# Adding the message bias of the first two pairs on GpSimd, and reordering the first loads, in a two-layer graph network kernel

## The chip, the cores and the metric

The kernel runs on one core of a Trainium2 chip, in one launch. A core has TensorE for matrix products (PE in the profile; its weight loads are shown apart as PEld), VectorE (DVE), ScalarE (ACT), GpSimd (POOL) and SyncE (SP, which here only issues DMAs). The metric is the device time of one execution in microseconds (us), as the median over several runs; less is better.

## What is computed

64 graphs of 256 nodes with 256 channels go through two layers. All data is float32. Layer 0 joins a convolution along the nodes, a message passing weighted by distance, and a gated recurrent unit; layer 1 is a graph convolution. Each ends in a residual and a normalisation. Cut to what matters:

```python
# layer 0
xc = jnp.transpose(x, (0, 2, 1))
h = relu(bn1(conv1d(xc, conv1_w, 0)))            # 1 tap
h = bn2(conv1d(h, conv2_w, 8))                   # 17 taps
x_conv = jnp.transpose(relu(h + xc), (0, 2, 1))
s = x @ w_se.T + b_se                            # 3 coordinates a node
dist = sq[:, :, None] + sq[:, None, :] - 2.0 * jnp.einsum('bnd,bmd->bnm', s, s)
A = jnp.exp(-dist) * mask                        # mask is adj
msg = relu(x @ w_msg.T + b_msg)
x_nmp = jnp.einsum('bnm,bmd->bnd', A, msg)
gi = concat([x_conv, x_nmp]) @ w_ih.T + b_ih;  gh = x @ w_hh.T + b_hh
r = sigmoid(gi_r + gh_r);  z = sigmoid(gi_z + gh_z);  nn_ = tanh(gi_n + r * gh_n)
x = _layernorm(x + (1.0 - z) * nn_ + z * x)
# layer 1
h = layer_norm(x, ln_gamma, ln_beta)
agg = jnp.einsum('bij,bjh->bih', adj, h)
x = _layernorm(x + x + relu(agg @ W_rel + b_rel + h @ W_root))
```

`sq` is the sum of the squares of `s`; `bn1` and `bn2` are a scale and a shift for each channel.

## The kernel before

**Staging.** The 64 graphs are worked on in 32 pairs, and the convolution in 8 batches of 4 pairs (`BG = 8` graphs). The 17-tap convolution is done in a transformed domain: a batch's activations (tile `XF`) go through butterflies on DVE (`split`, `merge`, lines 611 to 677), products with transformed filters on PE (`product`, L735), and butterflies back. The filters themselves are transformed at the start of the program (`filters`, lines 529 to 596): pieces of the filter weights are loaded (`wt`, L550), laid out by DVE (`ws`, L560), transposed on PE (L569), copied out by ScalarE (L571), multiplied with a small matrix (`ps_w`, L590) and copied into `w2all` by ScalarE (L596). Batch 0 uses `w2all` directly. It is also stored to DRAM (`w2m`, `store_w2`, L527), and from batch 1 on three filters at a time are loaded back into one of two buffers (`cs`, L728), whenever the products of the set before the last have read theirs.

**The first convolution** (`conv1`, 1 tap). For two graphs at a time `x` is loaded (L827), transposed on PE in two halves of the channels (L845, each half four transposes into one PSUM bank), copied out by ScalarE (L846), multiplied with the weights `w1` (L866), and scaled, shifted and passed through a ReLU by ScalarE (L870). The scale and shift come from the channel table `chan` by a few small instructions on DVE and GpSimd (lines 516 to 520). Batch 0's first convolution is the first work of the program. ScalarE issues the loads of `chan` (L494), `w1` (L495) and the small matrix `taps` (L499) in this order; SP issues those of `x`.

**A pair** (`pair(p)`). The message product has 260 columns for a tile of 128 nodes: 256 message channels, 3 coordinates and one of zeros. `xT` times `wms` takes two products, over the two halves of the channels (L1105), into one PSUM bank. The bias `bms` is a tile with the same 260 columns in every partition. For most pairs DVE adds it on the way out of PSUM (L1112). For pairs 0 and 1 (`idle`) a third product adds it, a row of ones times one row of the bias (L1108), and ScalarE copies the bank out (L1110). Then ScalarE takes the coordinates (L1114) and applies the ReLU (L1116), GpSimd makes the squared norms (lines 1119 to 1123), DVE transposes the coordinates (L1126), two DMA round trips place them (L1130, L1135), and the distance products follow (L1142), the exponential (L1146), the mask (L1149) and the sum over neighbours (L1156). The convolution's result is `xc` (L930, L1162, L1163). The gates (L1194 for pairs 0, 1 and 31; L1208 for the others) multiply `xT`, the neighbour sums and `xc` with blocks `WB`, which for pair 0 are loaded (L1043) into the memory that `w2all` has given up. Layer 1 follows with L1383 and L1397.

**What sets the order.** The program is recorded as a list of operations, each with a key, and a planner (`scheduled`, lines 321 to 416) sorts them: it goes through time with assumed durations, DMA rates and PSUM banks, and gives each engine the ready operation of the smallest key. Keys come from the constants at the top: `FIRST_GATES` is the planned time of pair 0's gates and `PERIOD` that of a pair; the others place the loads, the convolution of the next batch, the coordinates (`COORDS`), layer 1's normalisation and projection (`W_LAG`, `LATE_LAG`), the filter stores (`STORES_AT`), or raise the priority of an operation on DVE (`PAIR_LEAD`, `FILTER_LEAD`). Each engine and each DMA queue then works in that fixed order and waits on semaphores. Any change of a constant or an operation can reorder all queues.

Of the kernel before, what the change touches and what calls it, by code (L numbers as in the profile page):

```python
# [18 lines left out]
P = 128  # L19
B, N, D = 64, 256, 256  # L20
C = D // P
# [10 lines left out]
BG = 8  # L32
# [22 lines left out]
OB, OG = 3, 64  # L55
HQ = 2 * M * C * (M + 1)
XC_SLOTS = BG + 2
FIRST_GATES, PERIOD, GATE_TIME = 115.6, 58.9, 14.5
AHEAD_FROM, AHEAD_TO, W_DEEP = -43.5, -52.5, 2
CONV1_FROM, CONV1_TO, CONV_FROM, CONV_OUT, CONV_TO = -29.4, 98.8, -11.5, -38.6, -37.2  # L60
PAIR_LEAD, FILTER_LEAD, LOAD_AHEAD = 40.6, -2.5, 17.5
SMALL_RUNS, TURN_FROM = 1.3, 2
FILTERS_TO, STORES_AT = 51.5, 52.7
KEEP = 13.3
LATE_LAG = 28.4
W_FROM, W_LAG = 2, 41.9
COORDS = 40.5
PLAIN, SUMS_FROM = (0, 1, B // 2 - 1), 2


# [349 lines left out]
def gnn_two_layers(  # L420
# [18 lines left out]
    prog = Program()  # L439
    PE, V, A, G, SP = prog.tensor, prog.vector, prog.scalar, prog.gpsimd, prog.sync  # L440
# [3 lines left out]
    def sb(name, shape, pool="const"):  # L444
        s = Space(name, shape, pool)
        s.after = opened.get(pool)
        spaces[pool].append(s)
        return s.view
# [4 lines left out]
    def bank(name, share="rest"):  # L453
        return Space(name, [P, 512], "psum", share, share if share in ("conv", "gate") else None).view
# [22 lines left out]
    w1 = sb("w1", [P, C, D])  # L477
    mhalf = sb("mhalf", [P, 8])
    ones = sb("ones", [P, P])
    ident = sb("ident", [P, P])  # L480
# [10 lines left out]
    taps = sb("taps", [P, NM * OB], "filters")  # L491

    prog.at(0.0)
    A.dma_start(out=chan_sb, in_=chan)  # L494
    A.dma_start(out=w1, in_=w1T.rearrange("(c p) n -> p c n", p=P))  # L495
    tb = np.zeros((2, OG, NM * OB), np.float32)
    tb[:, :TAPS * OB] = np.einsum("kf,op->kofp", tap_matrix(), np.eye(OB, dtype=np.float32)).reshape(TAPS * OB, NM * OB)
    tb = tb.reshape(P, NM * OB)
# [294 lines left out]
    def fold(q):  # L793
        g0, g1 = 2 * q, 2 * q + 2
        for j, r in ((0, 8), (8, 0)):
            hv = HP[:, q, j:j + 8].rearrange("p j c g k -> p (j c) g k")
            for first, op in ((V0 + r, ALU.subtract), (U + r, ALU.add)):
                o = sl(first, 8).rearrange("p s (c e) -> p (s c) e", c=C)[:, :, g0 * M:g1 * M]
                V.tensor_tensor(o.rearrange("p s (g t) -> p s g t", t=M), hv[:, :, :, 0:M], hv[:, :, :, 1:M + 1], op)

    def hd(p):
        return h_dram[p].rearrange("f p e -> (f p e)")[:P * HQ].rearrange("(p e) -> p e", p=P)

    def conv1(b):
        def edges(h):
            G.memset(h[:, :8, :, :, M:], 0.0)
            G.memset(h[:, 8:, :, :, :1], 0.0)
        XN = {}

        def fetch(g):  # L810
            if b >= TURN_FROM:
                XN[g] = xn_ahead[:, :4 * D]
                blocks = XN[g].rearrange("p (c k i) -> p c k i", c=C, i=SQ)
                rows_of = x[b * BG + g:b * BG + g + 2].rearrange("g (b j) d -> j (g b) d", j=SQ)
                with prog.group():
                    for a in range(P // SQ):
                        for c in range(C):
                            at = c * P + a * SQ
                            SP.dma_start(out=blocks[a * SQ:(a + 1) * SQ, c], in_=rows_of[:, :, at:at + SQ])
                return  # L820
            if b > 0:
                XN[g] = xn_ahead[:, :4 * D].rearrange("p (j d) -> p j d", d=D)
            elif g >= 4:
                XN[g] = W2[:, 1, 8 + 2 * g:12 + 2 * g]
            else:
                XN[g] = cs[:, g * 512:g * 512 + 1024].rearrange("p (j d) -> p j d", d=D)
            SP.dma_start(out=XN[g], in_=x[b * BG + g:b * BG + g + 2].rearrange("g (c p) d -> p (g c) d", p=P))  # L827

        def turned(g):
            xn = XN[g]  # L830
            if b >= TURN_FROM:
                V.transpose(xTc_ahead.rearrange("p c n -> p (c n)"), xn)
                SP.dma_start(out=xt_dram[(b * BG + g) // 2], in_=xTc_ahead)
                return xTc_ahead
            if b > 0 or g == 4:
                xTc = xTc_ahead
            elif g:
                xTc = W2[:, 1, 6 * g - 12:6 * g - 8].rearrange("p (c f) o -> p c (f o)", c=C)
            else:
                xTc = cs[:, 2048:3072].rearrange("p (c n) -> p c n", c=C)  # L840
            for c in range(C):
                ps = bank("ps_xTc")
                with prog.group():
                    for j in range(4):
                        PE.transpose(ps[:, j * P:(j + 1) * P], xn[:, j, c * P:(c + 1) * P], ident, hold=[xTc[:, c]])  # L845
                A.copy(xTc[:, c, :], ps)  # L846
            SP.dma_start(out=xt_dram[(b * BG + g) // 2], in_=xTc)
            return xTc

        if b == 0:  # L850
            for g in range(0, BG, 2):
                fetch(g)
                edges(HP[:, g // 2])
        for g in range(0, BG, 2):
            h = HP[:, g // 2]
            if b > 0:
                fetch(g)
            xTc = turned(g)
            if b > 0:
                h = xn_ahead.rearrange("p (j c g k) -> p j c g k", j=M, c=C, g=2)  # L860
                edges(h)
            for o in range(C):
                ps = bank("ps_c1")
                with prog.group():
                    for c in range(C):
                        PE.matmul(ps, w1[:, c, o * P:(o + 1) * P], xTc[:, c, :], start=(c == 0), stop=(c == C - 1),  # L866
                                  hold=[h[:, :, o]])
                pv = ps.rearrange("p (g t j) -> p j g t", g=2, j=M)
                for j, at in ((0, 0), (8, 1)):
                    A.activation(h[:, j:j + 8, o, :, at:at + M], pv[:, j:j + 8],  # L870
                                 AF.Relu, bias=bn_shift[0][:, o:o + 1], scale=bn_scale[0][:, o:o + 1])
            if b == 0:
                fold(g // 2)
            else:
                SP.dma_start(out=hd(b * BG // 2 + g // 2), in_=xn_ahead)
# [88 lines left out]
    bms = sb("bms", [P, D + 4])  # L964
# [38 lines left out]
    msg = sb("msg", [P, 2, C, D + 4], "ahead")  # L1003
# [5 lines left out]
    def keep(steps, key):  # L1009
        for q in range(BG // 2):  # L1010
            prog.at(key + KEEP * q)
            next(steps, None)
# [44 lines left out]
    ps = bank("ps_hrow")  # L1057
# [10 lines left out]
    ps = bank("ps_mean")  # L1068
# [17 lines left out]
    def pair(p):  # L1086
# [12 lines left out]
        idle = p < 2  # L1099
        for g in range(2):  # L1100
            for m in range(C):
                ps = bank("ps_msg")
                with prog.group():
                    for c in range(C):
                        PE.matmul(ps[:, :D + 4], xT[:, c, g, m * P:(m + 1) * P], wms[:, c, :], start=(c == 0),  # L1105
                                  stop=(c == C - 1 and not idle), hold=[msg[:, g, m]])
                    if idle:
                        PE.matmul(ps[:, :D + 4], ones[0:1, :], bms[0:1, :], start=False, stop=True)  # L1108
                if idle:
                    A.copy(msg[:, g, m], ps[:, :D + 4])  # L1110
                    continue
                V.tensor_add(msg[:, g, m], ps[:, :D + 4], bms)  # L1112
        for m in range(C):
# [10 lines left out]

        prog.at(due - COORDS, 0.3)
        V.transpose(turned.rearrange("p m e -> p (m e)"), st.rearrange("p m e -> p (m e)"))  # L1126
        placed = s_dram[p % 2].rearrange("q (f n) -> (q f) n", n=N)[:16]
        with prog.group():
            for a in range(P // SQ):
                SP.dma_start(out=placed.rearrange("f (m b i) -> f m b i", m=C, i=SQ)[:, :, a, :],  # L1130
                             in_=turned[a * SQ:a * SQ + 16])
# [5 lines left out]
        pss = [bank("ps_dist") for _ in range(2 * C)]  # L1137
        with prog.group():
            for g in range(2):
                for m in range(C):  # L1140
                    r = slice((2 * g + m) * SR, (2 * g + m) * SR + 4)
                    PE.matmul(pss[2 * g + m][:, :N], lr[r, 0, m * P:(m + 1) * P], lr[r, 1, :], start=True, stop=True,  # L1142
                              hold=[AT[:, g, m]])
# [7 lines left out]
        for g in range(2):  # L1151
            ps = bank("ps_nmp")
            with prog.group():
                for d in range(C):
                    for m in range(C):
                        PE.matmul(ps[:, d * N:(d + 1) * N], msg[:, g, m, d * P:(d + 1) * P], AT[:, g, m, :],  # L1156
                                  start=(m == 0), stop=(m == C - 1), hold=[nmp[:, :, g]])
# [100 lines left out]
        else:  # L1258
            for T in (RG, ZN):
# [10 lines left out]
                d = bank("ps_d", "gate")  # L1270
# [17 lines left out]
        for some in pieces:  # L1288
            r, gh, z, n = (T[:, some, h, :] for T in (RG, ZN) for h in range(2))
# [77 lines left out]
        def project(gs, q):  # L1367
            prog.at(due + 2 * GATE_TIME + (8 if not apart else -6 if gs[0] else 13 - 2 * GATE_TIME) + (0.0 if apart or p < W_FROM else LATE_LAG if late else W_LAG), 0.6)
            if apart:
# [17 lines left out]
        def aggregate(gs):  # L1387
            prog.at(due + 2 * GATE_TIME + (16 if not apart else 14 - 2 * GATE_TIME) + (0.0 if apart or p < W_FROM else LATE_LAG if late else W_LAG), 0.4)
            q, sh = next(q3s), next(shs)
# [71 lines left out]
    for b in range(NB):  # L1461
# [11 lines left out]
        if b + 1 < NB:  # L1473
            start, span = FIRST_GATES + b * BG // 2 * PERIOD, BG // 2 * PERIOD
# [99 lines left out]
```

## Time and profile before

| | us |
|---|---|
| median of 3 runs (1989.74 to 1990.74) | 1990.72 |
| the profiled execution's own time | 1990.39 |
| its span, first to last instruction | 1988.6 |
| PE busy | 1974.2 |
| DVE busy | 1710.0 |
| ScalarE busy | 1006.7 |
| GpSimd busy | 275.3 |
| one-row products (L1108), 16 passes, busy | 5.6 |
| mean granted TensorE clock | 0.999 |

A float32 product appears as two passes, so the 8 one-row products are 16 rows on PE. A timeline line has start, duration, engine, line, operation, output and inputs, shape and count; in brackets stand the idle time before it and what ended that. A line of a stretch has its bounds, its length, and the busy time of PE, PEld, DVE, ACT and POOL with their counts, then the granted clock, the busy share of the DMA engines and GB/s. SPq and ACTq are the times that an engine's queue took to issue a DMA; when a transfer has landed is read from the sixteen semaphore updates that each makes. Busy times overlap, and idle time of an engine that does not set the end costs nothing.

### The profile page before, as it was taken

The numbers are of one execution on the slowest core, as the hardware profiler recorded it, in microseconds if no ns is written. First come the engines' busy times: TensorE is split into PE (matmuls) and PEld (weight loads), VectorE is DVE, ScalarE is ACT, GpSimd is POOL, SyncE is SP. The second block draws the span as 40 slices with busy tenths as digits, with TensorE's granted clock in tenths as the row PEclk, the third lists the DMA queues.
The fourth block names the chain that finished last, engine by engine and source line by source line (L and its number), as shares of the span: only waits on it lengthen the run. The fifth ranks groups of instructions, "written<-read, shape, count | busy, mean of one in ns | idle before, by whom it ended". The sixth has DMA issues, their size and how long they took to land.

```text
span 1988.6 us, 28895 instructions
## 1 busy us (share of the span) xinstructions
PE 1974.2 (99%) x10212; PEld 1604.6 (81%) x10212; DVE 1710.0 (86%) x2674; ACT 1006.7 (51%) x2342; POOL 275.3 (14%) x504
## 2 busy tenths in 40 slices
PE   9999999999999999999999999999999999999998
PEld 6887789777887788878887788877888788887875
DVE  6896998999989999899998999899988999985655
ACT  7545342754456543475345644475444653465432
POOL 1000110210110211111110111111111021111101
PEclk9999999999999999999999999999999999999999
DMA  8954555446545465445553545544554334422221
GB/s 219 309 169 127 139 170 140 126 108 186 136 141 149 110 184 143 130 132 135 184 153 109 142 140 171 146 136 112 156 149 150 99 84 158 126 77 77 76 54 43
DMA packets 461089, 273.14 MB, mean 137 GB/s; under 512 B 258192, under 2 KB 445584, under 8 KB 460944
## 3 DMA queue, kind: packets, MB, share of 16 engines
q1 hardware_dynamic: 460384, 270.94, 47.1%
q8 instruction: 81, 1.33, 0.3%
q14 instruction: 64, 0.52, 0.1%
q10 hardware_dynamic: 560, 0.34, 0.1%
HBM read 194.01 MB, written 77.20 MB: 136 GB/s over the span
## 4 chain that ended last, share of the span: by engine, by line
PE 97%; ACT 1%; DVE 1%; DMA 1%; issue 0%; SPq 0%; POOLq 0%; POOL 0%; ACTq 0%; DVEq 0%
PE ps_a L1208 22%; PE ps_k L735 17%; PE ps_d L1208 11%; PE ps_hy L1383 11%; PE ps_c L866 6%; PE ps_nmp L1156 6%; PE ps_msg L1105 6%; PE ps_b L1208 6%; PE ps_agg L1397 5%; PE ps_g L1194 5%; PE ps_dist L1142 1%; ACT w2all L596 1%; PE ps_w L590 1%; ACT tT L571 0%; DMA w<-in_w1T_dram 0%
## 5 line engine op out<-in xcount | busy, mean ns | idle before, releaser
L735 PEld LDWEIGHTS ps_k<-XF,cs 128*128 128x128 f32 x2632 | 311.8, 192 | 14.7 <-issue 8.7
L735 PE MATMUL ps_k<-XF,cs 128*128 128x128 f32 x2632 | 313.3, 275 | 0.0
L1383 PE MATMUL ps_hy<-wrr,wT 128*128 128x512 f32 x496 | 226.8, 595 | 0.0
L1208 PE MATMUL ps_a<-nmp,WB 128*128 128x256 f32 x696 | 207.0, 379 | 0.0
L1383 PEld LDWEIGHTS ps_hy<-wrr,wT 128*128 128x128 f32 x496 | 91.6, 190 | 89.8 <-issue 83.0
L1208 PE MATMUL ps_a<-tx,WB 128*128 128x256 f32 x522 | 156.0, 381 | 2.0 <-ACT ZN L1220 2.0
L1222 ACT ACTIVATE RG<-ps_a,bhh 128x512 f32<-128x512 f32 x116 | 79.2, 683 | 142.8 <-PE ps_a L1208 140.6
L1208 PEld LDWEIGHTS ps_a<-nmp,WB 128*128 128x128 f32 x696 | 132.2, 190 | 18.0
L1220 ACT COPY ZN<-ps_a 128x512 f32<-128x512 f32 x116 | 67.6, 582 | 149.4 <-PE ps_a L1208 148.8
L707 DVE TENSOR_TENSOR XF<-XF 128x512 f32<-128x512 f32 (+3 forms) x128 | 125.8, 1002 | 10.0 <-ACT XF L788 8.6
L1105 PE MATMUL ps_msg<-wms,xT 128*128 128x260 f32 x512 | 133.2, 383 | 0.0
L1156 PE MATMUL ps_nmp<-AT,msg 128*128 128x256 f32 x512 | 118.8, 379 | 0.0
L1385 DVE SCALAR_TENSOR_TENSOR HY<-ps_hy,q,hrow 128x512 f32<-128x512 f32 x124 | 92.7, 748 | 30.2 <-PE ps_hy L1383 24.9
L1397 PE MATMUL ps_agg<-HY,adja 128*128 128x256 f32 x504 | 117.2, 379 | 0.0
L1208 PEld LDWEIGHTS ps_a<-tx,WB 128*128 128x128 f32 x522 | 96.5, 190 | 24.7 <-issue 9.3
L1397 PEld LDWEIGHTS ps_agg<-HY,adja 128*128 128x128 f32 x504 | 95.1, 190 | 23.6 <-issue 10.9
L1156 PEld LDWEIGHTS ps_nmp<-AT,msg 128*128 128x128 f32 x512 | 96.8, 190 | 15.9 <-issue 2.9
L1105 PEld LDWEIGHTS ps_msg<-wms,xT 128*128 128x128 f32 x512 | 94.7, 190 | 14.9 <-issue 2.6
L866 PE MATMUL ps_c<-xTc,w 128*128 128x512 f32 x232 | 105.9, 594 | 0.0
L1208 PE MATMUL ps_a<-xc,WB 128*128 128x256 f32 x348 | 103.5, 379 | 0.0
L1208 PE MATMUL ps_a<-tc,WB 128*128 128x256 f32 x348 | 103.5, 379 | 0.0
L1208 PE MATMUL ps_d<-nmp,WB 128*128 128x256 f32 x348 | 103.5, 379 | 0.0
(226 smaller groups left out, 4254.7 us busy)
## 6 DMA issues: line engine op xcount, KB each, us to landing
cs<-w2m SPq DMA_DIRECT2D x105, 768.0 KB
adjm<-in_adjT_dram SPq DMA_DIRECT2D x64, 256.0 KB
xT<-xt SPq DMA_DIRECT2D x32, 512.0 KB
adja<-in_adjT_dram SPq DMA_DIRECT2D x64, 256.0 KB
out_dram<-HY SPq DMA_DIRECT2D x63, 256.0 KB
hd<-xn SPq DMA_DIRECT2D x28, 544.0 KB
XF<-hd SPq DMA_DIRECT2D x28, 544.0 KB
xt<-xTc SPq DMA_DIRECT2D x29, 512.0 KB
```

What stands on the lines that cost most here:

```text
L707: (V.tensor_add if add else V.tensor_sub)(sl(o, n), sl(a, n), sl(b, n))
L735: PE.matmul(ps[:, o * P:(o + 1) * P], w(m, c)[:, o * P:(o + 1) * P], X[:, slot, c * P:(c + 1) * P], start=first and o == 0 and c == 0, sto ...
L866: PE.matmul(ps, w1[:, c, o * P:(o + 1) * P], xTc[:, c, :], start=(c == 0), stop=(c == C - 1), hold=[h[:, :, o]])
L1105: PE.matmul(ps[:, :D + 4], xT[:, c, g, m * P:(m + 1) * P], wms[:, c, :], start=(c == 0), stop=(c == C - 1 and not idle), hold=[msg[:, g, m]])
L1156: PE.matmul(ps[:, d * N:(d + 1) * N], msg[:, g, m, d * P:(d + 1) * P], AT[:, g, m, :], start=(m == 0), stop=(m == C - 1), hold=[nmp[:, :, g]])
L1194: PE.matmul(ps[:, h * N:(h + 1) * N], block[:, s, gate, :], right[s][2 * k + g], start=0 in ks and h == 0 and s == sources[0] and k == 0, ...
L1208: PE.matmul(ps[:, h * N:(h + 1) * N], block[:, s, gate, :], right[s][at], start=start and h == 0 and j == 0, stop=j == len(sources) - 1, s ...
L1220: A.copy(o, ps)
L1222: A.activation(o, ps, AF.Identity, bias=bhh[:, 2, f:f + 1])
L1383: PE.matmul(ps, wT[:, 2 * f + g, m * P:(m + 1) * P], wrr[:, f, :], start=(f == 0), stop=(f == C - 1), hold=[HY[:, g, m]], need=[q[:, 1, j: ...
L1385: stt(HY[:, g, m, :], ps, q[:, 1, j:j + 1], hrow)
L1397: PE.matmul(ps[:, n_ * D:(n_ + 1) * D], adja[:, g, m, n_ * P:(n_ + 1) * P], HY[:, g, m, :D], start=(m == 0), stop=(m == C - 1))
```

## The change

Four things change. For pairs 0 and 1 the one-row product is gone: ScalarE copies the bank out, and GpSimd then adds the bias in SBUF, one instruction of 128x260 for each of the eight tiles. The load of `w1` is issued ahead of that of `chan`. The load of the first two graphs of `x` is split into one for each graph, and their transposes are grouped by graph, so that each of two PSUM banks gets two transposes from the first graph and two from the second; both copies follow. And eleven of the planner's constants have new values, which reorders the queues of all engines through most of the program.

```diff
-FIRST_GATES, PERIOD, GATE_TIME = 115.6, 58.9, 14.5
-AHEAD_FROM, AHEAD_TO, W_DEEP = -43.5, -52.5, 2
+FIRST_GATES, PERIOD, GATE_TIME = 112.8, 58.9, 14.5
+AHEAD_FROM, AHEAD_TO, W_DEEP = -31.4, -60.1, 2
...
-PAIR_LEAD, FILTER_LEAD, LOAD_AHEAD = 40.6, -2.5, 17.5
+PAIR_LEAD, FILTER_LEAD, LOAD_AHEAD = 40.4, 0.1, 17.5
...
-FILTERS_TO, STORES_AT = 51.5, 52.7
-KEEP = 13.3
-LATE_LAG = 28.4
-W_FROM, W_LAG = 2, 41.9
-COORDS = 40.5
+FILTERS_TO, STORES_AT = 51.4, 46.6
+KEEP = 13.0
+LATE_LAG = 28.1
+W_FROM, W_LAG = 2, 43.3
+COORDS = 39.9
...
+    A.dma_start(out=w1, in_=w1T.rearrange("(c p) n -> p c n", p=P))
     A.dma_start(out=chan_sb, in_=chan)
-    A.dma_start(out=w1, in_=w1T.rearrange("(c p) n -> p c n", p=P))
...
-            SP.dma_start(out=XN[g], in_=x[b * BG + g:b * BG + g + 2].rearrange("g (c p) d -> p (g c) d", p=P))
+            for k in range(2) if b == 0 and g == 0 else ():
+                SP.dma_start(out=XN[g][:, 2 * k:2 * k + 2], in_=x[k].rearrange("(c p) d -> p c d", p=P))
+            if b > 0 or g > 0:
+                SP.dma_start(out=XN[g], in_=x[b * BG + g:b * BG + g + 2].rearrange("g (c p) d -> p (g c) d", p=P))
...
-            for c in range(C):
+            if b == 0 and g == 0:
+                pss = [bank("ps_xTc") for _ in range(C)]
+                for k in range(2):
+                    with prog.group():
+                        for c in range(C):
+                            for j in (2 * k, 2 * k + 1):
+                                PE.transpose(pss[c][:, j * P:(j + 1) * P], xn[:, j, c * P:(c + 1) * P], ident,
+                                             hold=[xTc[:, c]])
+                for c in range(C):
+                    A.copy(xTc[:, c, :], pss[c])
+            for c in range(C) if b > 0 or g > 0 else ():
...
-                                  stop=(c == C - 1 and not idle), hold=[msg[:, g, m]])
-                    if idle:
-                        PE.matmul(ps[:, :D + 4], ones[0:1, :], bms[0:1, :], start=False, stop=True)
+                                  stop=(c == C - 1), hold=[msg[:, g, m]])
                 if idle:
                     A.copy(msg[:, g, m], ps[:, :D + 4])
+                    G.tensor_add(msg[:, g, m], msg[:, g, m], bms)
                     continue
```

## The prediction

> **What bounds the kernel now.** I read the page's busy times and chain first, then stretches of the span, the list of who waited for whom, and the timelines of the places that the diff touches.
>
> ```profile
> PE 1974.2 (99%) x10212; PEld 1604.6 (81%) x10212; DVE 1710.0 (86%) x2674; ACT 1006.7 (51%) x2342; POOL 275.3 (14%) x504
> PE 97%; ACT 1%; DVE 1%; DMA 1%; issue 0%; SPq 0%; POOLq 0%; POOL 0%; ACTq 0%; DVEq 0%
> 60.00:90.00 30.00, 29.07 (x208) 22.98 (x206) 28.48 (x46) 12.65 (x31) 0.26 (x2) 1.00 1.06 351
> 90.00:120.00 30.00, 30.00 (x249) 27.64 (x248) 24.64 (x39) 10.54 (x22) 1.73 (x7) 1.00 0.29 101
> 600.00:1500.00 900.00, 900.00 (x4542) 732.45 (x4541) 814.32 (x1234) 466.01 (x1112) 133.75 (x240) 1.00 0.50 142
> ```
>
> The second number of a stretch is its length, the third PE's busy time, the fifth DVE's. PE never rests from 66 us to 1580 us, at a granted clock of 1.00, so an instruction taken off PE there is time taken off the end, as long as what feeds PE can come earlier too. PE's idle time is 14.4 us (1988.6 - 1974.2): some 3 us before 7.1 us, 1.3 us up to 66 us, 2 us between 1580 and 1950 us, the rest at the end. In the instruction order of the two built programs the last 231 merged rows of PE are equal, and 224 of DVE's, so I leave the end as it is.
>
> **The one-row products (L1108) go.** Four groups of two passes for each of pairs 0 and 1:
>
> ```profile
> 80.78 1.04 PE L1105 MATMUL ps_msg<-wms,xT 128*128 128x260 f32 x4
> 81.75 0.70 PE L1108 MATMUL ps_msg<-bms,ones 1*128 1x260 f32 x2
> 82.38 1.98 PE L866 MATMUL ps_c<-xTc,w 128*128 128x512 f32 x4
> ...
> 382.60 1.04 PE L1105 MATMUL ps_msg<-wms,xT 128*128 128x260 f32 x4
> 383.47 0.59 PE L1208 MATMUL ps_a<-xT,WB 128*128 128x256 f32 x2
> ```
>
> From start to start a message tile takes 1.60 us with the one-row product (80.78 to 82.38) and 0.87 us without it, as later pairs do (382.60 to 383.47). The difference, 0.73 us, is more than two more passes of the same width (0.43): PE's weight load also waits 0.34 us at the change of rows. 8 x 0.73 = **5.8 us** off a PE that is full.
>
> In their place come eight GpSimd adds of 128x260 behind ScalarE's copies. No such add is in the trace. Below, the nearest rows are 0.20 us (128x4 add beside an idle DVE), above 1.38 us (the 128x1536 memset, L543) and 1.79 us (the power of 128x8, L1358); I take 1.0 us, between them. They lie off PE: POOL is busy 1.7 us of 90 to 120 us. Behind them wait the coordinates of a pair (L1114 to L1135), then its distance products. Pair 0: last message tile copied at 89.8, distances at 118.0; the built order still leaves 27.5 us of PE work between. Pair 1: 30 us. One add in series is hidden in either, and would have to last over 5 us to show.
>
> **Weights and x at the start.**
>
> ```profile
> 1.18 0.55 ACTq L495 DMA_DIRECT2D w<-in_w1T_dram  x1
> 5.00 1.15 PE L845 MATMUL ps_xTc<-ident,cs 128*128 128x128 f32 x8
> 5.74 1.07 ACT L846 COPY cs<-ps_xTc 128x512 f32<-128x512 f32 x2 [2.10 <-PE ps_xTc L845]
> 7.07 3.67 PE L866 MATMUL ps_c<-cs,w 128*128 128x512 f32 x8 [0.92 <-DMA w<-in_w1T_dram]
> ```
>
> The first product could start when ScalarE's first copy ends (5.74 + 0.54 = 6.28) and waits for w1 until 6.93. With w1 issued at 0.72 this wait goes, and x is next: by the trace's semaphore events x's first 512 KB landed at 4.86, when by its DMA packets some 780 KB had moved in all, and w1 and the second x at 6.93 and 7.13, while 340 KB moved a microsecond. Now w1 is ahead of x's second half, which is issued 0.5 us later than the first (SP's issue takes 0.50). What the first product needs is then 776 KB with the channel table: that half lands at 4.86 if nothing later shares, at 5.61 (4.86 + 256/340) if it gets nothing before 4.86; I take 5.3, a little past the middle, as the second x and the taps are issued 0.5 us behind it. Both ScalarE copies now wait for its four transposes: 5.3 + 0.14 + 0.74 + 0.54 + 0.1 = 6.8. Gain **0.3 us**, ends -0.1 and 0.7. The channel table, now second, may land at 5.5 instead of 4.0; its chain (DVE, POOL's two powers, DVE) took 2.2 us and is needed 2 us after the first product, at 8.8: no cost, 1 us spare. On SP, the later x and filter loads move back by one issue, 0.5 us; the first of them is used 3 us after landing.
>
> **Order of the filter stage.** The new constants also reorder the queues. SP before:
>
> ```profile
> 45.41 3.23 SPq L527 DMA_DIRECT2D w2m<-w2all  x3
> 48.75 2.41 SPq L550 DMA_DIRECT2D wt<-in_w2T_dram  x1
> 60.31 0.64 DVE L560 COPY ws<-wt 128x612 f32<-128x612 f32 x2
> 62.74 0.99 PE L590 MATMUL ps_w<-taps,tT 51*128 51x141 f32 x12 [0.70 <-ACT tT L571]
> ```
>
> The last filter piece is loaded behind three 1 MB stores and lands at 58.80; DVE lays it out at 60.31, and PE (0.70) and ScalarE (0.69) both go idle behind that. In the built order this load is ahead of all stores (its buffer is free at about 45.2) and DVE's copy stands eight rows earlier. The wait goes; ScalarE is busy 98% of 25 to 60 us, so it may bind again at once: gain 0 to 0.7, I take **0.5 us**. The stores start some 0.5 us later; the first x of batch 1 landed at 70.20 for a use at 72.91 and pair 0's x at 72.95 for 76.46, spare 2.7 and 3.5 us, of which PE's lead of 0.8 and the 0.5 take half.
>
> **Can the feeders follow?** DVE waited 8.4 us for PE and ScalarE in 66 to 131 us (L773 5.1 in five, L707 2.0, L1126 0.7, L789 0.6). PE's work from its first conv product to batch 0's last is shorter by 4.5 us in the built order; with 0.8 already gained, 5.3 us, which DVE's waits hold. The first product with xc came 23.2 us after that last conv product (129.27 to 152.49), its operand 21.1 us after it (ScalarE's ReLU ended at 150.36). By the same prices the new order has 21.8 us there: spare 0.7. The gate weights (WB) start landing 2.8 us after the last conv product, and the first gate now comes 7.9 us after it, not 11.0; the two blocks that its first products need had landed 5.9 us after, spare 2.0. I put **+0.4 us** for waits that these thin margins let through, ends 0 and 4.
>
> **Sum.** -5.8 - 0.3 - 0.5 + 0.4 = -6.2 us: the span goes from 1988.6 to 1982.4. The profiled execution took 1990.39, 0.33 below the median of 1990.72, which becomes **1984.5**.
>
> **Rivals.** *GpSimd's adds hold up DVE.*
>
> ```profile
> 91.05 0.20 POOL L1121 TENSOR_TENSOR ns<-ns,sq 128x4 f32<-128x4 f32 x1
> 142.16 0.53 POOL L1121 TENSOR_TENSOR ns<-ns,sq 128x4 f32<-128x4 f32 x1
> ```
>
> The same GpSimd add takes 0.20 us while DVE is idle and 0.53 beside DVE's L924, which keeps its pace of 0.61. So they do meet, and here GpSimd gives way. If DVE gave way instead, pair 1's four adds would put 4 x 1.0 us into the DVE chain with 0.7 us spare: 3.3 us of PE idle before the first xc product, 1984.5 + 3.3 = 1987.8. The Trainium skill's SBUF — State Buffer, section Who interferes with whom, says that a DVE instruction with two SBUF inputs and a GpSimd instruction that reads SBUF lock each other out for the whole instruction, whoever starts first; by that rule either can be held, and the two rows show only GpSimd held. Chance 0.11.
>
> *DVE binds the first products.* DVE is busy 28.5 of 30 us in 60 to 90 us, where four of the eight groups go. If its conv combinations can't come earlier, those 2.9 us (4 x 0.73) are not gained: 1987.4. Against it: from 91 to 95 us DVE is idle 3.2 us for PE's product. Chance 0.11.
>
> *Slower: the last filter weights of each batch come late.* A batch's last products use buffers that are refilled when the products two sets before end. In five batches the built order leaves 7.0 us of PE work for that; before it was 10.4 and 11.3 in three of them, though 7.0 also occurs before, without a wait. The refills at 801.76 and 802.65 took 4.1 and 5.4 us from issue to landing, 0.3 us after release: 1.3 us spare. It decides from 7.9 us on (6.2/5 = 1.24 past 6.7). The longest refill in the trace, behind other loads at 378.36, took 9.1: (9.1 + 0.3 - 7.0) x 5 = 12 us, 1984.5 + 12 = 1996.5. Refills within a batch took up to 5.7. Chance 0.07.
>
> That the products stay is excluded: the built order has none from that line.
>
> **From this the numbers.** Forecast 0.70, with 1983.3 to 1986.5 as its own range; the rivals as above; 0.01 for the rest. 0.2% (4.0 us) is about what a measurement of this kernel tells from no change. Faster by more (under 1986.7): 0.70. Within: the two middle rivals, 0.21. Slower: 0.09, the third and unknown waits. The range goes down to 1983.0 (all gains at their best ends: -5.8 - 0.7 - 0.7) and up to 1989.5, over both middle rivals.
>
> **What would show it.** No one-row rows on PE, message groups 0.87 us apart; eight 128x260 adds on POOL; first product near 6.8; no PE wait near 62 us and conv products from about 64.7; first gate product near 132 instead of 140.3; PE full from there to 1573. It is wrong if PE shows a wait for DVE or ScalarE between 65 and 146 us, or one for a DMA of the filter weights once per batch.

## The result and the profile after

The changed kernel takes 1985.09 us (median of 11 runs, 1984.83 to 1986.80); the kernel before, on the same chip, 1989.87 us (11 runs, 1989.35 to 1990.77). The ratio is 0.9976, with a 95% interval of 0.9968 to 0.9984: 4.8 us faster, with 1984.5 forecast. The profiled execution took 1985.06 us; its span, first to last instruction, is 1983.3, and before it was 1988.6.

The page of the changed kernel, busy time by engine and the chain that ended last:

```profile
PE 1968.8 (99%) x10196; PEld 1602.8 (81%) x10196; DVE 1714.0 (86%) x2674; ACT 1009.2 (51%) x2342; POOL 290.8 (15%) x512
...
PE 96%; ACT 2%; DVE 1%; DMA 1%; issue 0%; SPq 0%; POOLq 0%; POOL 0%; DVEq 0%; ACTq 0%
```

PE still sets the time. It is busy 5.4 us less (1974.2 before) with 16 passes fewer, and idle as much as before: 14.5 us (1983.3 - 1968.8) against 14.4. But the idle time is not the same one. The list of PE's waits in the changed kernel (line and releaser, us in total, times, longest):

```profile
PE ps_agg L1448 <- ACT x L1376: 2.0, 1, 2.0
PE ps_a L1220 <- ACT ZN L1232: 2.0, 3, 0.7
PE ps_mean L1084 <- DVE wrr L1080: 1.4, 1, 1.4
PE ps_warm L507 <- DVE bms L994: 1.1, 1, 1.1
PE ps_w L590 <- ACT tT L571: 0.3, 1, 0.3
PE ps_c L879 <- ACT cs L853: 0.2, 1, 0.2
PE ps_xTc L850 <- DMA cs<-in_x_dram: 0.2, 1, 0.2
```

The waits for the last filter weights (0.7) and for w1 (0.9) are gone. One has come that counts: 1.4 us at L1084, for DVE's L1080. The two of 0.2 us at L879 and L850 are new too; they belong to the head, the stretch up to the first product. The other rows are those of before under new line numbers. From 147 to 1580 us PE waits for nothing. The timeline of the changed kernel, PE at the places that the prediction named:

```profile
7.24 1.98 PE L879 MATMUL ps_c<-cs,w 128*128 128x512 f32 x4 [0.25 <-ACT cs L853]
...
64.86 2.35 PE L735 MATMUL ps_k<-XF,w2all 128*128 128x128 f32 x17
...
80.23 1.04 PE L1118 MATMUL ps_msg<-wms,xT 128*128 128x260 f32 x4
81.11 2.84 PE L735 MATMUL ps_k<-XF,w2all 128*128 128x128 f32 x24
...
131.90 1.03 PE L1206 MATMUL ps_g<-xT,WB 128*128 128x256 f32 x4
...
145.59 1.96 PE L1084 MATMUL ps_mean<-wrr,ones 128*128 128x512 f32 x4 [1.41 <-DVE wrr L1080]
147.38 2.97 PE L1206 MATMUL ps_g<-xc,WB 128*128 128x256 f32 x13
```

Before, the same places, and the product at L1071 that is now L1084:

```profile
65.47 2.80 PE L735 MATMUL ps_k<-XF,w2all 128*128 128x128 f32 x21
...
150.78 1.88 PE L1071 MATMUL ps_mean<-wrr,ones 128*128 128x512 f32 x4
152.49 3.62 PE L1194 MATMUL ps_g<-xc,WB 128*128 128x256 f32 x16
```

The first product starts at 7.24 (before 7.07), the first conv product at 64.86 (65.47), a message tile takes 0.88 us from start to start, the first gate product comes at 131.90 (140.31), the first product with xc at 147.38 (152.49). From there to the start of the last adjacency group (L1448; 1974.23, before 1979.61) is 1826.85 us, before 1827.12. So the span's 5.3 us divide as: head +0.17, head to first conv product -0.78, conv product to xc product -4.50, from there to the last adjacency group -0.27, the end +0.08. The new wait lies in the conv product to xc product part.

### The profile page after: what moved, and what is told of

It reads as the page before. It is cut to its first block, busy times and chain, and to the rows that moved or that the text cites. A ratio compares the mean times of both kernels' runs of the same rounds, so it can differ in the third digit from the quotient of the medians.

```text
span 1983.3 us, 28889 instructions
## 1 busy us (share of the span) xinstructions
PE 1968.8 (99%) x10196; PEld 1602.8 (81%) x10196; DVE 1714.0 (86%) x2674; ACT 1009.2 (51%) x2342; POOL 290.8 (15%) x512
## 4 chain that ended last, share of the span: by engine, by line
PE 96%; ACT 2%; DVE 1%; DMA 1%; issue 0%; SPq 0%; POOLq 0%; POOL 0%; DVEq 0%; ACTq 0%
PE ps_a L1220 23%; PE ps_k L735 17%; PE ps_d L1220 11%; PE ps_hy L1395 11%; PE ps_b L1220 6%; PE ps_nmp L1168 6%; PE ps_agg L1409 5%; PE ps_msg L1118 5%; PE ps_c L879 5%; PE ps_g L1206 4%; PE ps_dist L1154 1%; ACT w2all L596 1%; ACT tT L571 1%; DMA cs<-w2m 0%; PE ps_hy L1386 0%
## 5 line engine op out<-in xcount | busy, mean ns | idle before, releaser
L707 DVE TENSOR_TENSOR XF<-XF 128x512 f32<-128x512 f32 (+3 forms) x128 | 126.6, 1010 | 8.5 <-ACT XF L788 6.6
L1168 PE MATMUL ps_nmp<-AT,msg 128*128 128x256 f32 x512 | 119.1, 379 | 0.0
L1409 PEld LDWEIGHTS ps_agg<-HY,adja 128*128 128x128 f32 x504 | 95.1, 190 | 25.7 <-issue 14.4
L1423 POOL TENSOR_SCALAR total<-total 128x4 f32<-128x4 f32 x28 | 13.4, 478 | 655.7 <-ACT HY L1419 640.1
L1168 PEld LDWEIGHTS ps_nmp<-AT,msg 128*128 128x128 f32 x512 | 96.8, 190 | 13.8 <-DVE AT L1161 0.5
L1118 PEld LDWEIGHTS ps_msg<-wms,xT 128*128 128x128 f32 x512 | 94.8, 190 | 14.5 <-issue 2.4
L879 PE MATMUL ps_c<-xTc,w 128*128 128x512 f32 x232 | 106.3, 593 | 0.0
```

Source lines behind the costliest of these rows:

```text
L707: (V.tensor_add if add else V.tensor_sub)(sl(o, n), sl(a, n), sl(b, n))
L1409: PE.matmul(ps[:, n_ * D:(n_ + 1) * D], adja[:, g, m, n_ * P:(n_ + 1) * P], HY[:, g, m, :D], start=(m == 0), stop=(m == C - 1))
```

## The experiments

All but one kernel below are the changed kernel with its planner's order kept: an instruction is dropped, added or moved after the planner has run, since any edit ahead of it would reorder every queue. Three starts from each trace, in us, read the places; the time is the median of all runs of that kernel, or its only run where one is given.

| kernel | first product | first conv product | first xc product | span | time |
|---|---|---|---|---|---|
| before | 7.07 | 65.47 | 152.49 | 1988.6 | 1989.87 (11) |
| changed | 7.24 | 64.86 | 147.38 | 1983.3 | 1985.09 (11) |
| no_adds | 6.84 | 64.45 | 145.32 | 1981.2 | 1983.20 (5) |
| rows_back | 7.12 | 64.73 | 151.71 | 1988.1 | 1989.68 (11) |
| x_whole | 6.87 | 64.48 | 146.99 | 1983.1 | 1985.97 (11) |
| moved799 | 7.04 | 64.66 | 147.18 | 1983.2 | 1984.97 (9) |
| adds_twice | 6.76 | 64.37 | 150.13 | 1987.8 | 1990.26 (1) |
| late_wt | 6.82 | 65.65 | 148.15 | 1984.1 | 1986.60 (10) |
| first1080 | 7.03 | 64.64 | 146.00 | 1982.1 | 1984.01 (7) |
| one_add | 7.28 | 64.89 | 147.51 | 1984.0 | 1985.32 (10) |
| dve_adds | 7.30 | 64.92 | 146.48 | 1982.4 | 1984.20 (1) |
| dve_first1080 | 6.88 | 64.49 | 145.38 | 1981.3 | 1983.14 (5) |
| old_head | 7.12 | 64.71 | 147.23 | 1983.5 | 1985.49 (1) |

The kernel before, on the chips of the three groups of runs (the first four, the next four, the last four with bias_only), took 1990.01, 1990.21 and 1990.96 us.

**no_adds: is it GpSimd that makes DVE late?**

```diff
         for name, method, args, named, line in op.calls:
+            if line == 1122:
+                continue
```

> The changed kernel in its own order with the eight GpSimd adds of the bias left out (the bias of the messages of pairs 0 and 1, an array of zeros here, is not added). Theory (the adds hold up DVE): DVE's L937 x8 falls from 5.98 us to about 4.9 and the L933 beside an add from 1.22 to 0.69, PE's 1.4 us wait for wrr (L1084) goes to 0.2 or less, the span is 1.2 to 1.4 us shorter, the time 1983.7. Rival (the new order alone makes DVE late): the wait stays at 1.2 to 1.4 us and the time at 1985.1.

It took 1983.20 us (1983.03 to 1983.78), ratio to before 0.9965 (0.9952 to 0.9977). PE has no wait at L1084. DVE's queue is the same row for row, so its timeline can be laid beside that of the changed kernel (start, duration, how many). The changed kernel:

```profile
124.41 2.73 DVE L707 TENSOR_TENSOR XF<-XF 128x256 f32<-128x256 f32 x4 [1.40 <-ACT XF L788]
...
128.96 1.30 POOL L1122 TENSOR_TENSOR msg<-msg,bms 128x260 f32<-128x260 f32 x1 [1.09 <-ACT msg L1121]
129.59 1.22 DVE L933 SCALAR_TENSOR_TENSOR XF<-XF 128x512 f32<-128x512 f32 x1
...
135.44 5.98 DVE L937 SCALAR_TENSOR_TENSOR XF<-XF 128x512 f32<-128x512 f32 x8
136.02 1.30 POOL L1122 TENSOR_TENSOR msg<-msg,bms 128x260 f32<-128x260 f32 x1 [5.76 <-ACT msg L1121]
139.49 0.79 POOL L1122 TENSOR_TENSOR msg<-msg,bms 128x260 f32<-128x260 f32 x1 [2.16 <-ACT msg L1121]
...
144.96 0.88 DVE L1080 TENSOR_SCALAR wrr<-wrr,gb 128x512 f32<-128x512 f32 x2
```

And no_adds:

```profile
124.00 2.28 DVE L707 TENSOR_TENSOR XF<-XF 128x256 f32<-128x256 f32 x4 [1.40 <-ACT XF L788]
...
128.74 0.68 DVE L933 SCALAR_TENSOR_TENSOR XF<-XF 128x512 f32<-128x512 f32 x1
...
134.05 4.90 DVE L937 SCALAR_TENSOR_TENSOR XF<-XF 128x512 f32<-128x512 f32 x8
...
142.49 0.88 DVE L1080 TENSOR_SCALAR wrr<-wrr,gb 128x512 f32<-128x512 f32 x2
143.60 1.88 PE L1084 MATMUL ps_mean<-wrr,ones 128*128 128x512 f32 x4
```

L933 beside one add takes 0.54 us more (1.22 - 0.68), L937 x8 beside two adds 1.08 more (5.98 - 4.90), L707 x4 beside pair 1's first add 0.45 more (2.73 - 2.28): together 2.07. Counted from the first product, L1080 starts at 137.72 in the one and at 135.65 in the other, 2.07 apart. So pair 1's four adds account for DVE's delay to the hundredth. L1084 itself starts 138.35 us after the first product with the adds and 136.76 without: 1.59 later, of which the list shows 1.41 as idle. What is left of 2.07, 0.48 us, is the slack that DVE had on the way to L1084. Pair 0's four adds held DVE for 1.9 us as well (in L640, L707, L651 and L653), but without them DVE waits for PE's products soon after; by L773 near 116 us both kernels stand level, 108.76 and 108.75 us after the first product. The theory holds; the rival falls.

GpSimd is held too: its row is 0.73 us where it starts as a DVE instruction ends, and 1.30 where the next one, 0.6 us long, was let through first. The Trainium skill, SBUF — State Buffer, section Who interferes with whom, says that a DVE instruction with two SBUF inputs and a GpSimd instruction that reads SBUF contend for one port pair, and that the one that issues second is blocked, not slowed; for these adds the trace agrees on both sides: DVE stands for 0.54 us, GpSimd for up to 0.57 (1.30 - 0.73).

**rows_back: what do the one-row products cost?**

```diff
+        if op.row is not None:
+            op.calls[-1][3]["stop"] = False
+            op.calls.append(("tensor", "matmul", (op.row, ones[0:1, :], bms[0:1, :]), {"start": False, "stop": True}, 1120))
         for name, method, args, named, line in op.calls:
+            if line == 1122:
+                continue
```

> The changed kernel in its own order with the one-row products back in PE's eight groups and no GpSimd adds. Theory (PE is full there, so a one-row product costs its 0.73 us): +5.8 for eight of them, less the 1.4 us wait that goes with the adds, +4.4: 1989.5, message tiles 1.60 us apart. Rival (DVE is what binds these stretches, the products partly fill waits): +2.9 or less, so 1986.6 or less after the wait is taken off.

1989.68 us (ratio 0.9997, 0.9988 to 1.0006), the time of before. Against no_adds, which differs by the eight products alone, the stretch from the first conv product to the first xc product grows from 80.87 to 86.98 us: 6.11, or 0.76 a product, and none of it fills a wait. The theory holds. Head, filter stage and constants together, with the products kept, show nothing in the time. The traces do show something: 57.61 us from the first product to the first conv product against 58.40 before, and 1.0 us less up to the last adjacency group (1978.57 against 1979.61). Half of that is lost again at the end, where the last adjacency group takes 3.54 us, at a granted clock of 0.50 from 1979.2 to 1982.6 us, and 2.17 before.

**x_whole and old_head: the head.** x_whole loads the first x at once again, with the transposes in their old order; old_head also puts the channel table ahead of the weights.

```diff
-            for k in range(2) if b == 0 and g == 0 else ():
-                SP.dma_start(out=XN[g][:, 2 * k:2 * k + 2], in_=x[k].rearrange("(c p) d -> p c d", p=P))
+            SP.dma_start(out=XN[g], in_=x[0:2].rearrange("g (c p) d -> p (g c) d", p=P))
```

> The changed kernel in its own order with the first x in one load again (weights still first) and its transposes in the old order, one chunk of four after the other. Theory (two loads share the engines with the next loads, so the second half lands about 1 us late): x lands near 4.9, the first copy ends near 6.3, the first product starts at 6.3 to 6.6 instead of 7.24, and 0.5 to 0.8 us of it reaches the end: 1984.4. Rival (what is loaded ahead of x, the weights, delays it): x lands at 5.6 or later, the first product at 7.0 to 7.3, no gain: 1985.1.

> The changed kernel in its own order with the head of before: the channel table loaded first, then the weights, the first x in one load. Theory (the head's change is worth nothing that exceeds its spread from run to run, 6.76 to 7.28 us over seven kernels with the new head): the first product at 6.8 to 7.3 us, with a wait for the weights. Rival (weights first gains): at 7.4 us or later.

By the semaphore events x landed at 5.43 us in x_whole, between the two cases, and at 4.80 in old_head; the weights at 5.14 and 6.99; in the changed kernel x's halves at 4.49 and 5.84 and the weights at 4.85. What lands first trades places, and the later of the two decides. In all ten traces with the split, x's second half lands at 5.56 to 6.12, later than the whole x in x_whole. The first product starts at 6.87 and 7.12. The changed kernel and the nine of the table that keep its head start it at 6.76 to 7.30 (mean 7.03), three kernels with the old head (before, old_head, and bias_only below) at 7.07, 7.12 and 7.26. Neither theory of x_whole is borne out cleanly, and for old_head the first one is: the head's change is inside its own spread. x_whole's runs spread more than most (1984.71 to 1987.58; their spans go from 1982.8 to 1985.5, with 1983.1 in the profiled one); why is not known.

**late_wt: the filter stage.** The last load of filter weights goes behind three stores, and DVE's two copies of it behind the second L707, by engine queues that are changed and then merged under the same dependencies.

```diff
+    q = seqs["SP"]
+    i = [k for k, o in enumerate(q) if o.line == 550][7]
+    q[i:i + 4] = q[i + 1:i + 4] + [q[i]]
+    q = seqs["DVE"]
+    move = [o for o in q if o.line == 560][8:10]
+    i = [k for k, o in enumerate(q) if o.line == 707 and k > q.index(move[1])][1]
+    q[:i + 1] = [o for o in q[:i + 1] if o not in move] + move
```

> The changed kernel in its own order, but the last load of filter weights again behind three of the 1 MB stores, and DVE's two copies of it behind the second L707 of 128x2048, as before the change. Theory (that load's place is what gained in the filter stage): PE waits 0.7 us near 62 us again, the first conv product is at 65.5 to 65.7 instead of 64.9, and 0.6 to 0.8 us reach the end: 1985.8. Rival (the gain came from the other reordered rows): the first conv product stays within 0.2 us of 64.9, the time at 1985.1.

1986.60 us (ratio 0.9983, 0.9974 to 0.9992). PE's waits between 55 and 70 us in late_wt:

```profile
PE ps_tT L569 <- DVE ws L560: 1.2, 1, 1.2
```

From the first product to the first conv product it took 58.83 us; in the changed kernel 57.62, in the kernel before 58.40. So the place of this load and of its two copies is worth 1.2 us in the new order, more than the 0.8 that the change gained there, and it shows at the end. The theory holds, at a larger size. The two are not told apart: the load lands at 58.55 and the copies start at 60.44, the moment that the L707 ahead of them in DVE's queue ends; before the change it was 58.80 and 60.31 in the same way.

**adds_twice and one_add: does DVE pay by time, by instruction or by columns?** adds_twice issues every add two times; one_add has one add of 128x1040 a pair, behind the pair's last copy.

```diff
-                one_line(line)(getattr(getattr(nc, name), method), [made(v) for v in args],
-                               {k: made(v) for k, v in named.items()})
+                for _ in range(2 if line == 1122 else 1):
+                    one_line(line)(getattr(getattr(nc, name), method), [made(v) for v in args],
+                                   {k: made(v) for k, v in named.items()})
```

```diff
+            if line == 1122:
+                if args[0].chain[-1][1][0][1:] == (1, 1):
+                    nc.gpsimd.tensor_add(made(msg), made(msg), made(bms).unsqueeze(1).unsqueeze(1).to_broadcast([P, 2, C, D + 4]))
+                continue
```

> The changed kernel in its own order with each of the eight GpSimd adds issued twice (the bias is added twice to the messages of pairs 0 and 1; it is an array of zeros here). Theory (DVE pays for the time that GpSimd's adds run beside it): DVE loses about as much again, PE's wait at L1084 goes from 1.4 to 2.8 to 3.4 us, the span to 1984.7 to 1985.3. Rival (only the first meeting of an add with a DVE instruction costs, or the adds hide in DVE's gaps): the wait stays at 1.4 to 1.8 us.

> The changed kernel in its own order with one GpSimd add of 128x1040 a pair, behind the pair's last copy, in place of four of 128x260. Theory (DVE pays by the time that GpSimd runs, and four short adds run longer than one wide one): the wide add takes 2 to 3 us against 4.1 for pair 1's four, DVE loses about half, the wait at L1084 is 0.7 us or less, the time 1984.3. Rival (DVE pays by the elements that GpSimd moves): DVE loses as much, the wait stays at 1.2 us or more, 1985.1.

adds_twice, DVE and then PE:

```profile
136.65 7.05 DVE L937 SCALAR_TENSOR_TENSOR XF<-XF 128x512 f32<-128x512 f32 x8
...
147.83 2.51 PE L1084 MATMUL ps_mean<-wrr,ones 128*128 128x512 f32 x4 [3.41 <-DVE wrr L1080]
```

The wait at L1084 is 3.41 us, 2.0 more than with four adds a pair, as the theory has it; L937 x8 takes 7.05, which is 4.90 and four times 0.54. Its span of 1987.8 is beyond what was expected. A further 0.5 us of wait, for DVE too, stands at L1168 ahead of the xc products (119.39 us). Right behind the long wait the granted clock is 0.50, from 149.1 to 152.5 us, and the sixteen first xc products take 4.79 us where they take 3.62 in the changed kernel; that is about what the stretch from the first xc product to the last adjacency group is longer by (1.2 us). No other trace here, with waits for DVE of up to 2.2 us, has such a dip before 1970 us, so the long wait is the likely cause, but one run alone shows it. In one_add the rival holds: the wait is 1.5 us and the time 1985.32 (ratio 0.9975, 0.9966 to 0.9984). Its timeline shows the price in one row:

```profile
134.49 4.90 DVE L937 SCALAR_TENSOR_TENSOR XF<-XF 128x512 f32<-128x512 f32 x8
139.42 3.50 DVE L799 TENSOR_TENSOR XF<-XF 128x512 f32<-128x512 f32 x2
139.53 2.84 POOL L1540 TENSOR_TENSOR msg<-msg,bms 128x1040 f32<-128x1040 f32 x1 [11.63 <-ACT msg L1121]
```

L937 is back at 4.90, and the two L799 that take 1.29 us in the other traces take 3.50: DVE stands still for 2.21 us while the wide add runs. That is 2.1 ns a column (2.21 / 1040), and 0.54 / 260 is 2.1 too. Fewer instructions save nothing on DVE. The Trainium skill's GPSIMD Engine Reference, section 3.1 Elementwise — side-by-side cycle accounting, gives 4497 ns for such an add of 2048 columns on GpSimd; an estimate from that figure is 2.2 ns a column. That is GpSimd's own time, and DVE's standstill here comes close to it; the GpSimd rows themselves are 2.7 to 2.8 ns a column (2.84 / 1040, 0.73 / 260).

**moved799 and first1080: where does the delay reach PE?** L1080 stands in DVE's queue behind two L799, L1076 to L1078 and L1174. moved799 takes the two L799 out of its way. first1080 puts L1080 first, then L1076, L1077, one L799 and L1174, and on ScalarE L1175 ahead of the fourth L943 (first1080's edit is shown).

```diff
+    q = seqs["DVE"]
+    i = [k for k, o in enumerate(q) if o.line == 1076][0]
+    p = q[i - 2:i + 6]
+    q[i - 2:i + 6] = [p[6], p[7], p[2], p[3], p[0], p[5], p[4], p[1]]
+    q = seqs["ACT"]
+    i = [k for k, o in enumerate(q) if o.line == 1175][0]
+    q[i - 1], q[i] = q[i], q[i - 1]
```

> The changed kernel with DVE's two L799 that stand ahead of L1076 moved behind L1080, nothing else in any queue changed. Theory (PE's wait at L1084 is DVE's queue, 1.3 us late): the 1.29 us of the pair come off it, the wait goes to about 0.1 and the time to 1983.8. Rival (DVE is short of time over the whole stretch, so the wait goes to the next product that needs DVE): the wait turns up at the xc or later products within 10 us and the time stays at 1985.1.

> The changed kernel with DVE's two L1080 moved ahead of the pair of L799, L1174 after one L799, and ScalarE's L1175 ahead of the fourth L943; PE's order is unchanged. Theory (the wait is one of queue order: L1080 needs none of what stands ahead of it): PE does not wait at L1084, the xc products follow with 0 to 0.3 us of wait, 1.1 to 1.4 us come off the end: 1983.8. Rival (after GpSimd's adds the whole chain L937, L943, L1174, L1175 is late): 0.8 us or more of wait turns up at the xc products, the gain is 0.6 us at most: 1984.5 or more.

moved799 took 1984.97 us (ratio 0.9974, 0.9964 to 0.9984) with the same wait of 1.41 us at the same place, which neither theory had. Its timeline tells why:

```profile
141.95 0.43 DVE L1078 TENSOR_SCALAR hrow<-hrow 128x512 f32<-128x512 f32 x1
143.62 1.23 DVE L1174 TENSOR_TENSOR xc<-xc,xT 128x1024 f32<-128x1024 f32 x1 [1.24 <-ACT xc L943]
144.76 0.88 DVE L1080 TENSOR_SCALAR wrr<-wrr,gb 128x512 f32<-128x512 f32 x2
```

L1174 waits 1.24 us for ScalarE's L943, which starts only when L937 ends, and L1080 stands behind it though it needs neither. The L799 had filled time that was idle anyway. In first1080, L1080 passes L1174:

```profile
143.80 1.88 PE L1084 MATMUL ps_mean<-wrr,ones 128*128 128x512 f32 x4
146.00 3.72 PE L1206 MATMUL ps_g<-xc,WB 128*128 128x256 f32 x16 [0.32 <-ACT xc L1175]
```

PE goes into L1084 without a wait and waits 0.32 us for xc; the time is 1984.01 us (ratio 0.9970, 0.9959 to 0.9981). The theory holds: queue order carried the delay to PE, and 1.1 of the 1.41 us could be had back by a new order of nine instructions.

**dve_adds and dve_first1080: the same add on DVE.**

```diff
-                one_line(line)(getattr(getattr(nc, name), method), [made(v) for v in args],
+                one_line(line)(getattr(getattr(nc, "vector" if line == 1122 else name), method), [made(v) for v in args],
```

> The changed kernel in its own order with the eight adds of the bias on DVE at the same places of the order, instead of on GpSimd. Theory (a GpSimd add takes 0.54 us from DVE, 2.08 ns a column, so the same add is cheaper on DVE itself): a DVE add of 128x260 takes 0.35 to 0.45 us, DVE loses 0.1 us an add less, PE's wait at L1084 is 0.8 to 1.1 us instead of 1.41. Rival (in DVE's queue an add also waits for ScalarE's copy and holds all behind it): the wait is 1.4 us or more, and PE waits in other places of 75 to 146 us too.

> The kernel first1080 (L1080 ahead of L799, L1175 ahead of the fourth L943) with the eight adds on DVE at the same places. Theory (DVE loses less by its own adds than by GpSimd's): the 0.32 us of wait at the xc products goes too, 1983.7. Rival (DVE's queue waits for ScalarE's copies): new waits on PE before 146 us, 1984.5 or more.

dve_adds' timeline, where one add stands among L937:

```profile
135.11 1.89 DVE L937 SCALAR_TENSOR_TENSOR XF<-XF 128x512 f32<-128x512 f32 x3
136.91 0.42 DVE L1122 TENSOR_TENSOR msg<-msg,bms 128x260 f32<-128x260 f32 x1
137.25 3.09 DVE L937 SCALAR_TENSOR_TENSOR XF<-XF 128x512 f32<-128x512 f32 x5
```

The add takes 0.42 us, of which the next instruction overlaps 0.08 (136.91 to 137.25): 0.34 of DVE's time against the 0.54 that GpSimd's add takes from it. PE's wait at L1084 falls to 0.45. That is 0.96 less, where 4 x 0.20 makes 0.80; the rest is not accounted for, and this kernel ran once. Without L1080's detour as well, no wait is left between 65 us and 1580 us: dve_first1080 takes 1983.14 us (1983.08 to 1983.98), ratio 0.9961 (0.9948 to 0.9973). No kernel here takes less; no_adds, which leaves the bias out, takes 1983.20.

**bias_only: what were the constants for?** This is the kernel before with the bias part of the diff alone; its planner makes a new order from the old constants.

> The kernel of before with the bias part of the change alone: its constants and its head stay, and its planner makes the order from them. Theory (the products' 6.5 us reach the end but for what GpSimd's adds take from DVE, and the new constants were worth the 0.8 us of the filter stage): one wait of 1 to 2 us for DVE near the first xc products, PE's 0.7 us near 62 us still there, 1985.3 to 1986.0. Rival (with the old constants the order leaves the adds where they cost more, or DVE binds the first products): waits of 3 us or more between 65 and 155 us, 1987 or more.

1999.70 us (1997.66 to 2000.32), ratio 1.0042 (1.0028 to 1.0055): slower than before. PE is busy 1970.1 us, 4.1 less than before, and idle 25.6 (span 1995.7), 11.2 more. The head of the list of its waits:

```profile
PE ps_nmp L1155 <- DVE AT L1148: 4.8, 3, 2.2
PE ps_a L1207 <- ACT ZN L1219: 2.8, 3, 1.5
PE ps_agg L1435 <- ACT x L1363: 2.0, 1, 2.0
PE ps_wT L1337 <- DVE wT L1298: 1.8, 1, 1.8
PE ps_k L735 <- DMA cs<-w2m: 1.6, 2, 1.4
PE ps_hy L1382 <- ACT AT L1145: 1.4, 1, 1.4
```

Between 160 and 400 us alone PE stands for 8.0 us (240 - 232.03 busy), where before and in the changed kernel it stands for none. The rival was right in kind, but put the waits too early: the first stretch, up to 160 us, has 1.0 us of them that count. The last GpSimd add starts at 140.0, so these waits belong to the order and not to adds that run beside them. Which of the eleven constants takes them away was not tried.

## Why the prediction came out

The forecast was 1984.5 us for 1985.09, inside its own range, and the sum of -6.2 stood against a span that fell by 5.3. That it came so close is in part luck. It was counted from 1990.72, the median of three runs, where the eleven runs beside the changed kernel gave 1989.87; the medians fell by 4.8, not 6.2. And errors cancelled: products and filter stage gave 0.6 us more than forecast, head and feeders took 1.7 more. By its terms:

- **One-row products, -5.8.** Right. They were worth 6.1 (rows_back against no_adds), 0.76 each for 0.73.
- **Head, -0.3.** Not seen: +0.17 in the profiled run, within a spread of 0.5 us that the same head shows. The step that failed is the landing of x's second half, put at 5.3 with 5.61 as the bound; it was 5.84, and 5.56 to 6.12 in all ten traces with this head. With the weights first, the whole x had landed at 5.43 (x_whole), so no gain of the split shows.
- **Filter stage, -0.5.** Right in cause, -0.78 in size, and late_wt shows the place of that load and of its copies on DVE carrying it. ScalarE did not bind at once.
- **Can the feeders follow, +0.4.** Mis-sized: +1.65 (the stretch from first conv product to first xc product is 82.52 us with the adds and 80.87 without; 1.59 of it has come by the start of L1084). This term was off most. It worked out a spare time, 0.7 us, for the operand of the first xc product alone (1.05 in no_adds, where L1175 ends at 144.27 and that product starts at 145.32). The wait came one group of products earlier, at L1084, which it doesn't name and where DVE had 0.48. The flaw is what was said of GpSimd: "here GpSimd gives way", from one 128x4 add beside L924 that took 0.53 instead of 0.20. Such an add is too short to show what it takes from DVE (4 columns at 2.1 ns are 0.01 us), and the row was read as the rule. Pair 1's adds took 2.07 us from DVE in that stretch.
- **GpSimd's adds, hidden off PE.** They are, as work: 0.73 to 1.30 us each, around the 1.0 assumed, and nobody waits for them by more than 0.2 us. Their cost came by way of DVE, not of the coordinates.

These terms as measured, -6.1 + 0.17 - 0.78 + 1.65, with -0.27 and +0.08 in the rest of the program, make -5.25 for -5.3.

Of the rivals, the first (GpSimd's adds hold up DVE) had the mechanism and half the price: 1.4 us of PE idle where it said 3.3, since an add holds DVE for 0.54 us, not for the 1.0 that it was taken to last on GpSimd. It is the rule of the Trainium skill that was set beside it, and these adds follow it. The second (DVE binds the first products) did not happen: all of the products' time came off. The third (late refills) did not either; PE has no wait for a filter-weight DMA. That waits for DVE could show between 65 and 146 us was named as what would make the prediction wrong, and one did, at 145.59 us; without it the gain would have been larger by that much, an estimate. What no rival held is that the constants guard the order: with the old ones the bias edit loses 9 us (bias_only).

One end of its range does not follow from its own terms: with all gains at their best the sum is -7.2, which gives 1983.5 and not 1983.0. The result does not turn on it.

## What to carry to other kernels

Moving a two-input SBUF add from PE to GpSimd takes it off PE, but beside a busy DVE it is not free work: here it cost DVE 0.54 us where DVE's own add costs 0.34, so ask first whether DVE can do it itself. When a chain is late, look at which instruction of its queue needs none of what stands ahead of it; the wait at L1084 went when L1080 was put first, and not when other work was cleared out of its way. And where a planner orders the program, an edit's price is that of the built order: price the edit and the constants apart, by a kernel that keeps the one and drops the other.

## What the runs showed of the hardware that was not expected

A GpSimd add of 128x260 stops DVE's two-input SBUF instructions for 0.54 us and one of 128x1040 for 2.21, 2.1 ns a column in both, however the columns are cut. The other way round GpSimd can be held much longer than by one DVE instruction: L1131 (128x12) takes 0.20 us at its shortest, and in the changed kernel 2.51 us, from 147.00 until DVE's run of six L799 ends at 149.44, and the next GpSimd row starts only at 149.59; in moved799, beside eight, 3.71. The adds of L1122 got in after one L937 at most (1.30 against 0.73 us), and one_add's wide add after one L799. Why L1131 is shut out for the length of a run and these are not stays open. And the first product's start, set by DMA landings, varied from 6.76 to 7.30 us between kernels with the same head.
